# Two cross-attention layers: the first layer's leftover scalings on Pool, its maxima and sums stored from Pool's queue and loaded a fifth of a period later

## The chip, the cores and the metric

The kernel runs on one core of a Trainium2 chip. A time is the device time of one execution in microseconds (us); for the kernel before it is the median of three runs, for one of which (the profiled execution) there is also a trace. All arithmetic is in 32-bit floats. The engines are named as in the profile: PE does matmuls (its weight loads are listed as PEld), DVE and ACT are the vector and scalar engines, POOL (GpSimd) is a third engine for elementwise work that also issues DMAs, and SP only issues DMAs. PE and DVE/ACT share the accumulators in PSUM; everything else is in SBUF or, outside the core, in DRAM.

## The reference, cut to what matters

Eight batches, 100 rows of `x` with 640 columns, and a context of 722 rows with 1024 columns, the first 77 of which are text and the other 645 "ip". Two layers, each with 20 heads of 32 columns. The first layer is

```python
q = _split_heads(hidden_states @ Wq.T, H)
k = _split_heads(text @ Wk.T, H);        v = _split_heads(text @ Wv.T, H)
out_text = _merge_heads(_attend(q, k, v, sm_scale))        # softmax over 77
k_ip = _split_heads(ip @ Wk_ip.T, H);    v_ip = _split_heads(ip @ Wv_ip.T, H)
out_ip = _merge_heads(_attend(q, k_ip, v_ip, sm_scale))    # softmax over 645
return (out_text + out_ip) @ Wo.T + bo + residual
```

The second layer has the same shape with other weights; before its ip softmax it adds one bias per row and ip token, the same for all heads, and it multiplies the ip probabilities by a mask per row.

## The kernel before, in words

**Units and periods.** A unit `u` is one layer of one batch (0 to 7 the first layer, 8 to 15 the second). It is done in five chunks `c` of four heads (4 x 32 = 128 columns, the partitions of a tile). The main loop runs over the 80 pairs `(u, c)` in `ORDER`; one turn is a *period*, 11 to 33 us long. The first layer's 40 periods run from about 406 to 1380 us; ahead of them lies a preamble with all of `q` and the text's `k` and `v`.

**What a period does.** `scores` (line 982) multiplies the four heads' `q` with their keys in two parts: columns 0 to 511 (part 0), then 512 to 721 (part 1: the last 133 ip columns, then 77 of text). Rows (the 100 queries) lie on partitions. `maxima` (L1007) and `text_maxima` (L1028) reduce on DVE, `exponentials` (L1021) run on ACT and also sum. Then `factors` (L1043 to L1047) works out the sums, their reciprocals (`rz`, L1046) and the factors `mul` of the two parts. What comes after the maxima isn't emitted at once: it is put in a list, `later`, from which `emit` takes one entry ahead of each piece of other work, and all that is left at the period's end. In the period that follows, the probabilities are transposed by PE (`transposes`, L1147), copied out of PSUM, and multiplied with the values (`values`, L1173), after which the next period's scores begin.

**Other work in the same period.** Between those steps stand pieces of *production*: the products that make keys and values of the next pair of batches (`psk`, L669, and `psv`, L639). Each is done by seven products instead of eight (`seven`): every product's PSUM bank is emptied by an addition on DVE (L209, L219, L224, L230, L235) or a copy on ACT (L204, L213), and two banks are there for them. Their results (`ko`, `vo`) go out to DRAM by DMAs that Pool issues (`k_d`, L693 and L696; `v_d`, L654). `between(n, a, b, small)` emits the production that is planned between the fractions `a` and `b` of period `n`, with the small pieces in `small` (output and query projections) spread in it; `at[0]` to `at[3]` are a period's lists of those.

**What is special in the first layer.** Of the 722 columns, the first 384 (`KT` = 3 blocks of 128) are exponentiated only for their sums. Their transposed probabilities are made again in the next period, without a transpose: `key_scores` (L1123) multiplies keys with queries the other way round, `key_exponentials` adds the row maximum on DVE (L1130) and exponentiates on ACT (L1135). For that, each query's maximum must lie along the free axis of all partitions, and the same holds for the reciprocal sum, by which `values` multiplies at the end (L1179). So `finished` writes rows 8 and 9 of the small tile `st` (maxima and reciprocal sums, 100 partitions x 8 numbers) to DRAM, `st_d`, by one DMA of SP (L1075), and `load_stats` reads them back in the next period, broadcast, by five DMAs of SP (L1111 once, L1113 four times), into columns of `p` that nothing else reads. The other columns, 384 to 721, are scaled in `finished` by three DVE multiplications: 384 to 511 (L1069), 512 to 644 (L1061) and 645 to 721 (L1057), and are transposed in the next period: blocks 3 and 4 at four tenths of it, block 5 near its end.

**What sets the order.** The instructions of PE, DVE and ACT run in the order in which the program emits them (`PINNED`). Those of SP and Pool are ordered by a scheduler that knows what each waits for; each queue then runs in its order, and an instruction that waits holds up what is behind it. The loop around the change, as far as it is needed:

```python
first = last and last[0] < B          # the period before was one of layer 0
if first:
    load_stats(*last)
between(n, 0.0, 0.4, at[0])
if last:
    transposes(*last, KT if first else 0)
    transposes(*last, KT + 1 if first else 1)
between(n, 0.4, 0.5 if first else 0.6, at[1])
...
scores(u, c, 1, last if first else None)      # with key_scores of the period before
```

Of the kernel before, what the change touches and what calls it, by code (L numbers as in the profile page):

```python
# [11 lines left out]
ALU = mybir.AluOpType  # L12
AX = mybir.AxisListType

P = 128
B = 8
S = 100
# [3 lines left out]
NI = 645  # L21
NL = NI - 5 * P
NK = NI + NT
KA = 512
# [3 lines left out]
NC_ = C // P  # L28
NCC = CC // P
NTAIL = NL + NT  # L30
KT = 3
# [16 lines left out]
def two_layer_xattn(  # L48
# [17 lines left out]
    nc = tc.nc  # L66
# [20 lines left out]
    st_d = [dram.tile([2, 4, S], F32, tag=f"st_{i}", name=f"st_d{i}") for i in range(2)]  # L87
# [172 lines left out]
    with ExitStack() as es:  # L260
# [40 lines left out]
        for g in range(B // 2):  # L301
            t = fp.tile([P, 2, NC_, S], F32, tag="q", name=f"q0_{g}", bufs=2)
            ps = [product_ps(f"psq_{g}_{i}") for i in range(3)]
            for k in range(NC_):
                for c in range(NC_):
                    at = c % 2 * 2 * S
# [5 lines left out]
            for i in range(3):  # L312
                n = 2 if i < 2 else 1
# [178 lines left out]
    def load_q(u):  # L492
        l, b = divmod(u, B)
        t = tpool.tile([P, NC_, S], F32, tag="q", name=f"q_{u}")
        nc.sync.dma_start(t, q_d[l][b // 2][:, b % 2])
        qs_[u] = t

    def load_vt(u):
        l, b = divmod(u, B)
        t = tpool.tile([NTAIL, C], F32, tag="vt", name=f"vt_{u}")  # L500
        nc.sync.dma_start(t[:NL], vl_d[l][b * NL : (b + 1) * NL, :])
        nc.sync.dma_start(t[NL:], vt_d[l][b * NT : (b + 1) * NT, :])
        vts[u] = t

    def load_k(u, c):

        l, b = divmod(u, B)
        t = kpool.tile([P, NK], F32, tag="k", name=f"k_{u}_{c}")
        nc.sync.dma_start(t[:, :NI], k_d[u][:, c, :])
        nc.sync.dma_start(t[:, NI:], kt_d[l][c][:, b * NT : (b + 1) * NT])  # L510
        ks[u, c] = t

    def load_v(u, c):
        t = vpool.tile([P, NB, P], F32, tag="v", name=f"v_{u}_{c}")
        nc.sync.dma_start(t, v_d[u].rearrange("(j p) n -> p j n", p=P)[:, :, c * P : (c + 1) * P])
        vs[u, c] = t
# [457 lines left out]
    def emit(n):  # L974
        for _ in range(n):
            later.pop(0)[1]()
# [5 lines left out]
    def scores(u, c, part, keys_of=None):  # L982
# [18 lines left out]
        p, st, l = pr[u, c], stats[u, c], u // B  # L1001
        n = min(k1, NI) - k0
        lo, f, rz, mul = st[:, 8, :], st[:, 6:8, :], st[:, 9:11, :], st[:, 11:13, :]
# [38 lines left out]
        def factors():  # L1042
            nc.vector.tensor_reduce(st[:, 5, :], p[:, :, NI:], AX.X, ALU.add)  # L1043
            nc.vector.tensor_tensor(st[:, 3:5, :], st[:, 3:5, :], f, ALU.mult)
            nc.vector.tensor_tensor(st[:, 4, :], st[:, 3, :], st[:, 4, :], ALU.add)
            nc.vector.reciprocal(rz, st[:, 4:6, :])  # L1046
            nc.vector.scalar_tensor_tensor(  # L1047
                mul, f, mask_sb[:, l : l + 1], rz[:, 0:1, :].to_broadcast([S, 2, 4]), ALU.mult, ALU.mult
            )
# [5 lines left out]
        def scaled_rest(text):  # L1055
            if text:
                nc.vector.tensor_tensor(  # L1057
                    p[:, :, NI:], p[:, :, NI:], rz[:, 1, :].unsqueeze(2).to_broadcast([S, 4, NT]), ALU.mult
                )
            else:  # L1060
                nc.vector.tensor_tensor(  # L1061
                    p[:, :, KA:NI], p[:, :, KA:NI], mul[:, 1, :].unsqueeze(2).to_broadcast([S, 4, NI - KA]),
                    ALU.mult,
                )

        def finished():

            factors()
            nc.vector.tensor_tensor(  # L1069
                p[:, :, KT * P : KA], p[:, :, KT * P : KA],  # L1070
                mul[:, 0, :].unsqueeze(2).to_broadcast([S, 4, KA - KT * P]), ALU.mult,
            )
            scaled_rest(False)
            scaled_rest(True)
            nc.sync.dma_start(st_d[(NC_ * u + c) % 2].rearrange("r i q -> q r i"), st[:, 8:10, :])  # L1075

        for h in range(2):
            maxima(h)
# [29 lines left out]
    def load_stats(u, c):  # L1108

        whole, src = wholes[u, c], st_d[(NC_ * u + c) % 2]  # L1110
        nc.sync.dma_start(whole[:, :, :S], src[0].unsqueeze(0).to_broadcast([P, 4, S]))  # L1111
        for i in range(4):
            nc.sync.dma_start(  # L1113
                whole[32 * i : 32 * i + 32, :, S : S + S // 4],
                src[1, i].rearrange("(a q) -> a q", a=4).unsqueeze(0).to_broadcast([32, 4, S // 4]),
            )
# [203 lines left out]
    def loads(n):  # L1320
        u, p = divmod(n, NC_)
        if u % 2 == 0 and 0 < u <= LAST[0]:
            g = u // 2 - 1
            if p == 0 and u < LAST[0]:
                load_wo("o", wo[PAIRS[g][0] // B], g)
            if p == 1 and g < B // 2:
                load_wo("q", wq[1], g)
        if NC_ * LAST[0] + 1 <= n < NC_ * LAST[0] + 1 + NC_:
            load_wo("o", wo[1], len(PAIRS) - 2, [n - NC_ * LAST[0] - 1])
        if n == NC_ * LAST[0] + 2:  # L1330
            load_res(len(PAIRS) - 1)
        elif p == 0 and u % 2 == 1 and u < LAST[1]:
            load_res(u // 2)
        if p == 2 and u + 1 <= LAST[0]:
            load_vt(u + 1)
            load_q(u + 1)
            if u + 1 >= B:
                load_sem(u + 1)
                load_g(u + 1)
        if n == NC_ * LAST[0] - 1:  # L1340
            load_sem(LAST[1])
            load_g(LAST[1])
        if n == NC_ * LAST[0] + 1:
            load_vt(LAST[1])
        if n == len(ORDER) - 4:
            last_out_weights()

    with tc.manual_schedule(engines=PINNED):
        made_ahead = pair_tasks(PAIRS[0])
        todo = production()  # L1350
        at = pair_marks[PAIRS[0]]["k 4"] - 2
        made_ahead[at:at] = first_sums[PAIRS[1]]
        for _, f in made_ahead:
            f()
        load_q(0)
        load_vt(0)
        load_k(0, 0)
        done = [0]

        def next_task():  # L1360

            if todo[done[0]][0] and later:
                emit(1)
            todo[done[0]][2]()
            done[0] += 1

        def make(until):
            while done[0] < len(todo) and todo[done[0]][1] < until:
                next_task()

        mark = [0]

        def apart(until):

            while done[0] < len(todo) and todo[done[0]][1] < until and not any(
                t for t, _, _ in todo[mark[0] : done[0]]
            ):
                next_task()
            mark[0] = done[0]

        def between(n, a, b, small):

            mark[0] = done[0]
            near = 0.7 if n < NC_ * LAST[0] + 2 else 0.1
            for i, (_, f) in enumerate(small):
                make(n + a + (b - a) * (i + 1) / (len(small) + 1))
                apart(n + b + near)
                f()
            make(n + b)
            apart(n + b + near)  # L1390

        make(0.0)
        last = None
        for n, (u, c) in enumerate(ORDER):
            at = small_work(n)
            loads(n)
            scores(u, c, 0)
            if n == len(ORDER) - 1:
                load_v(*last)
                load_v(u, c)  # L1400
            first = last and last[0] < B
            if first:
                load_stats(*last)
            between(n, 0.0, 0.4, at[0])
            if last:
                transposes(*last, KT if first else 0)
                transposes(*last, KT + 1 if first else 1)
            between(n, 0.4, 0.5 if first else 0.6, at[1])
            if last and not first:
                transposes(*last, 2)  # L1410
                transposes(*last, 3)
            scores(u, c, 1, last if first else None)
            if n == NC_ * LAST[0] - 1:
                load_q(LAST[1])
            few = n >= NC_ * LAST[0] + 4
            if not few:
                between(n, 0.5 if first else 0.6, 0.8, at[2])
            if n < len(ORDER) - 2:
                load_v(u, c)
            if n + 1 < len(ORDER):  # L1420
                load_k(*ORDER[n + 1])
            if last:
                if not first:
                    transposes(*last, 4)
                transposes(*last, 5)
            if few:
                between(n, 0.6, 0.8, at[2])
            between(n, 0.8, 1.0, at[3])
            emit(len(later))
            if last:  # L1430
                values(*last)
            last = (u, c)
        last_out(0, [NC_ - 1])
        for j in range(6):
            transposes(*last, j, at_end=True)
        last_out_add(0)
        values(*last)
        last_out(1, [NC_ - 1])
        last_out_add(1)
# [46 lines left out]
```

## Time and profile before

| | |
|---|---|
| median of three runs | 2072.13 us (2071.38 to 2072.56) |
| the profiled execution | 2071.46 us, of which the span from first to last instruction 2069.7 |
| PE | 2023.6 us busy, 98% of the span |
| DVE | 1174.0 us, 57% |
| ACT | 716.0 us, 35% |
| POOL | 274.9 us, 13% (issuing DMAs and a few elementwise instructions) |
| the three scalings L1069, L1061, L1057 | 0.693, 0.708 and 0.471 us each; 40, 40 and 40 times in the first layer (the last two also in the second) |
| SP's write of `st_d` (L1075) | 40 times, 0.3 us to issue |
| SP waiting for that write to land, ahead of L1111 | 266.5 us in 40 waits, the longest 9.5 |

A line of the profile names a group of instructions by engine, line of the kernel, operation, and the tiles that it writes and reads. A timeline line begins with start and duration in us; in brackets stands how long the engine was idle before and what ended that. A time of PE's matmuls has a modelled end. In the lines of stretches, the columns are the stretch, its length, the busy time of PE, PEld, DVE, ACT and POOL with the number of instructions, the granted clock of PE, the DMA engines' share and GB/s. A group's line ends with count, busy time, mean duration in ns, and the idle time ahead of it with its main releasers.

### The profile page before, as it was taken

The numbers are of one execution on the slowest core, as the hardware profiler recorded it, in microseconds if no ns is written. First come the engines' busy times: TensorE is split into PE (matmuls) and PEld (weight loads), VectorE is DVE, ScalarE is ACT, GpSimd is POOL, SyncE is SP. The second block draws the span as 40 slices with busy tenths as digits, with TensorE's granted clock in tenths as the row PEclk, the third lists the DMA queues.
The fourth block names the chain that finished last, engine by engine and source line by source line (L and its number), as shares of the span: only waits on it lengthen the run. The fifth ranks groups of instructions, "written<-read, shape, count | busy, mean of one in ns | idle before, by whom it ended". The sixth has DMA issues, their size and how long they took to land.

```text
span 2069.7 us, 40047 instructions
## 1 busy us (share of the span) xinstructions
PE 2023.6 (98%) x15642; PEld 1560.7 (75%) x15642; DVE 1174.0 (57%) x3127; ACT 716.0 (35%) x2125; POOL 274.9 (13%) x433
## 2 busy tenths in 40 slices
PE   9999999999999999999999989999999999999998
PEld 9676767776776867778667867777777778889876
DVE  2223322256565465655657656655665667778787
ACT  1001000123333232223322333334544455566675
POOL 0002212111111111111111000101010101111110
PEclk9999999999999999999999999999999999999999
DMA  9544323334543755437466564536242536545461
GB/s 341 154 132 147 96 74 95 94 87 91 121 106 79 173 104 120 99 98 164 103 150 156 136 136 107 120 102 187 88 128 81 150 93 174 146 134 153 120 185 52
DMA packets 373050, 262.66 MB, mean 127 GB/s; under 512 B 123198, under 2 KB 342002, under 8 KB 372862
## 3 DMA queue, kind: packets, MB, share of 16 engines
q1 hardware_dynamic: 350814, 191.57, 38.2%
q0 software_dynamic: 21776, 68.44, 9.8%
q8 instruction: 123, 2.02, 0.5%
q14 instruction: 65, 0.53, 0.1%
q10 hardware_dynamic: 272, 0.10, 0.0%
HBM read 190.98 MB, written 69.06 MB: 126 GB/s over the span
## 4 chain that ended last, share of the span: by engine, by line
PE 60%; DVE 6%; DMA 3%; ACT 2%; issue 1%; SPq 0%; ACTq 0%; DVEq 0%
PE psv_d L639 5%; PE psv_a L639 5%; PE pspt L1147 5%; PE psk_a L669 5%; PE sc L996 5%; PE psk_d L669 4%; PE pv L1173 4%; PE pso L906 3%; PE psv_e L639 3%; PE psv_c L639 2%; PE psk_b L669 2%; PE psk_c L669 2%; PE psv_b L639 2%; PE psk_e L669 2%; PE psq L925 1%; DMA st_d<-st 1%
## 5 line engine op out<-in xcount | busy, mean ns | idle before, releaser
L1021 ACT ACTIVATE p<-sc,st 100x512 f32<-100x512 f32 (+1 forms) x320 | 165.9, 531 | 207.4 <-DVE st L1007 194.6
L1021 ACT ACTIVATE p<-p,st 100x512 f32<-100x512 f32 (+1 forms) x320 | 177.4, 556 | 75.7 <-DVE st L1013 75.6
L639 PE MATMUL psv_a<-wv,x 128*128 128x397 f32 (+1 forms) x560 | 185.5, 473 | 0.4 <-DVE ko L230 0.3
L639 PE MATMUL psv_d<-wv,s 128*128 128x320 f32 (+1 forms) x560 | 176.4, 458 | 3.4 <-ACT vo L213 2.3
L1154 DVE COPY pt<-pspt 128x400 f32<-128x400 f32 x239 | 132.9, 568 | 71.8 <-PE pspt L1147 69.7
L1147 PEld LDWEIGHTS pspt<-ident,p 100*128 100x128 f32 (+1 forms) x1440 | 141.9, 137 | 37.4 <-issue 4.9
L1147 PE MATMUL pspt<-ident,p 100*128 100x100 f32 (+1 forms) x1440 | 162.4, 251 | 6.9 <-DVE pt L1154 2.1
L693 POOL DMA_DIRECT2D k_d<-ko x140 | 100.3, 720 | 469.8 <-DVE ko L230 401.5
L1007 DVE TENSOR_REDUCE st<-sc 100x2 f32<-100x1024 f32 (+1 forms) x160 | 125.2, 824 | 54.1 <-PE sc L1123 39.6
L639 PEld LDWEIGHTS psv_a<-wv,x 128*128 128x128 f32 x560 | 103.4, 190 | 67.1 <-issue 10.4
L1013 DVE CUSTOM_DVE_ANT_0 p<-sc,sem 100x512 f32<-100x512 f32 (+1 forms) x320 | 138.7, 491 | 22.1 <-PE sc L996 20.5
L639 PEld LDWEIGHTS psv_d<-wv,s 128*128 128x128 f32 x560 | 104.4, 191 | 55.3 <-ACT vo L213 3.0
L669 PE MATMUL psk_d<-s,wk 128*128 128x256 f32 (+1 forms) x672 | 137.6, 350 | 6.0 <-DVE ko L224 4.0
L996 PE MATMUL sc<-k,q 32*100 32x210 f32 (+1 forms) x1280 | 139.9, 502 | 3.2 <-DMA k<-k_d 2.2
L669 PE MATMUL psk_a<-x,wk 128*128 128x256 f32 (+1 forms) x672 | 135.7, 347 | 1.8 <-ACT ko L204 1.0
L1135 ACT ACTIVATE pt<-pt 128x600 f32<-128x600 f32 x80 | 55.8, 705 | 228.7 <-DVE pt L1130 228.7
L669 PEld LDWEIGHTS psk_d<-s,wk 128*128 128x128 f32 x672 | 108.0, 189 | 27.1 <-DVE ko L224 5.4
L1152 ACT COPY pt<-pspt 128x400 f32<-128x400 f32 x121 | 59.5, 492 | 191.6 <-PE pspt L1147 191.5
L669 PEld LDWEIGHTS psk_a<-x,wk 128*128 128x128 f32 x672 | 109.1, 189 | 20.4 <-issue 4.2
L654 POOL DMA_DIRECT2D v_d<-vo x70 | 38.9, 556 | 634.6 <-DVE gst L629 320.3
L1053 ACT ACTIVATE p<-p,st 100x512 f32<-100x512 f32 x158 | 102.9, 715 | 27.4 <-DVE st L1047 27.1
L639 PE MATMUL psv_e<-wvt,x 128*128 128x397 f32 (+1 forms) x280 | 93.1, 474 | 0.0
(225 smaller groups left out, 3544.8 us busy)
## 6 DMA issues: line engine op xcount, KB each, us to landing
x<-ip_t SPq DMA_DIRECT2D x80, 512.0 KB
k<-k_d SPq DMA_DIRECT2D x80, 322.5 KB
v<-v_d SPq DMA_DIRECT2D x80, 320.0 KB
v_d<-vo POOLq DMA_DIRECT2D x70, 320.0 KB, 2.8
k_d<-ko POOLq DMA_DIRECT2D x112, 128.0 KB, 5.2
o<-wo SPq DMA_DIRECT2D x35, 320.0 KB
x<-ip_t SPq DMA_DIRECT2D x20, 532.0 KB
p<-st_d SPq DMA_DIRECT2D x40, 200.0 KB
```

The costliest lines, as they stand in the source:

```text
L639: nc.tensor.matmul(ps[:, :m], lhsT=tokens(k)[:, :P], rhs=w[:, k, :], start=(k == 0 and not go_on), stop=(k == HK - 1), skip_group_check=True,)
L669: nc.tensor.matmul(ps[:, i * m : (i + 1) * m], lhsT=w[:, k, :], rhs=tokens(k), start=(i == 0 and k == 0 and not go_on), stop=(k == HK - 1) ...
L693: nc.gpsimd.dma_start(dst[:, :, r], src)
L906: nc.tensor.matmul(ps[:, :cols], lhsT=wos["o", g, c][:, k, :], rhs=hsg[g][:, :n, k, :], start=(k == 0), stop=(k == NC_ - 1),)
L996: nc.tensor.matmul(scs[i // 2][:S, i % 2, : k1 - k0], lhsT=qs_[u][rows, c, :], rhs=ks[u, c][rows, k0:k1], start=True, stop=True)
L1007: nc.vector.tensor_reduce(st[:, part, 2 * h : 2 * h + 2], scs[h][:S, :, :n], AX.X, ALU.max, negate=True)
L1013: nc.vector.tensor_tensor_reduce(out=p[:, i, k0 : k0 + n], in0=scs[h][:S, i % 2, :n], in1=sems[u][:, k0 : k0 + n], scale=-1.0, scalar=3.0e ...
L1021: nc.scalar.activation(dst, dst if l else scs[h][:S, i % 2, :n], AF.Exp, bias=st[:, part, i : i + 1], scale=-1.0 if l else 1.0, accum_out= ...
L1053: nc.scalar.activation(p[:, i, :KA], p[:, i, :KA], AF.Copy, scale=mul[:, 0, i : i + 1])
L1147: nc.tensor.transpose(ps[:rows, i * S : (i + 1) * S], pr[u, c][:, i, j * P : j * P + rows], ident[:S, :S])
L1154: nc.vector.tensor_copy(dst, src)
L1173: nc.tensor.matmul(ps[32 * i : 32 * i + 32, q0 : q0 + S], lhsT=lhs, rhs=pt[:rows, j, i * S : (i + 1) * S], start=(j == 0 or apart and j == ...
```

## The change

In `finished`, which only the first layer uses, the three multiplications go from DVE to Pool; the DMA that writes the maxima and reciprocal sums to DRAM goes from SP's queue to Pool's, ahead of the multiplications. In the main loop, the five loads of `load_stats` are emitted after the production of the period's first fifth and the first small piece, instead of at the period's start. Nothing else differs, and the second layer is untouched.

```diff
         def finished():

             factors()
-            nc.vector.tensor_tensor(
-                p[:, :, KT * P : KA], p[:, :, KT * P : KA],
-                mul[:, 0, :].unsqueeze(2).to_broadcast([S, 4, KA - KT * P]), ALU.mult,
-            )
-            scaled_rest(False)
-            scaled_rest(True)
-            nc.sync.dma_start(st_d[(NC_ * u + c) % 2].rearrange("r i q -> q r i"), st[:, 8:10, :])
+            nc.gpsimd.dma_start(st_d[(NC_ * u + c) % 2].rearrange("r i q -> q r i"), st[:, 8:10, :])
+            for a, b, by in ((KT * P, KA, mul[:, 0, :]), (KA, NI, mul[:, 1, :]), (NI, NK, rz[:, 1, :])):
+                nc.gpsimd.tensor_tensor(
+                    p[:, :, a:b], p[:, :, a:b], by.unsqueeze(2).to_broadcast([S, 4, b - a]), ALU.mult
+                )
...
             first = last and last[0] < B
             if first:
+                between(n, 0.0, 0.2, at[0][:1])
                 load_stats(*last)
-            between(n, 0.0, 0.4, at[0])
+                between(n, 0.2, 0.4, at[0][1:])
+            else:
+                between(n, 0.0, 0.4, at[0])
```

## The prediction

> **What bounds the kernel now.** I read the page first, for the share of each engine, then busy time by stretches, then the timeline around each stop of PE in the first layer, then the waits of SP's own queue, and last the rows of Pool.
>
> ```profile
> span 2069.7 us, 40047 instructions
> PE 2023.6 (98%) x15642; PEld 1560.7 (75%) x15642; DVE 1174.0 (57%) x3127; ACT 716.0 (35%) x2125; POOL 274.9 (13%) x433
> ```
>
> PE bounds the whole. A change that leaves its matmuls alone, as this one does, can win only PE's idle time, and only where the first layer runs, about 406 to 1380 us. The stretches show how much that is; the second figure is PE's busy time:
>
> ```profile
> 400.00:700.00 300.00, 292.20 (x2146) 214.15 (x2145) 170.34 (x399) 89.04 (x287) 45.82 (x75) 1.00 0.41 96
> 700.00:1000.00 300.00, 296.26 (x2258) 222.05 (x2257) 173.60 (x405) 94.16 (x302) 41.33 (x66) 1.00 0.55 128
> 1000.00:1180.00 180.00, 174.69 (x1394) 134.16 (x1393) 114.19 (x254) 54.95 (x174) 23.71 (x38) 1.00 0.58 130
> 1180.00:1310.00 130.00, 120.39 (x966) 90.55 (x965) 77.89 (x180) 43.44 (x141) 11.81 (x18) 0.97 0.58 129
> 1310.00:1380.00 70.00, 69.25 (x584) 52.69 (x583) 47.70 (x125) 27.83 (x90) 6.15 (x10) 1.00 0.46 115
> ```
>
> Idle is 7.80 + 3.74 + 5.31 + 9.61 + 0.75 = 27.2 us. That is the most that can be won, 1.3%. What the moved DVE work has to do with it is seen in the timeline at 810 us:
>
> ```profile
> 810.25 0.70 DVE L1069 TENSOR_TENSOR p<-p,st 100x512 f32<-100x512 f32 x1
> 810.85 0.71 DVE L1061 TENSOR_TENSOR p<-p,st 100x532 f32<-100x532 f32 x1
> 811.48 0.47 DVE L1057 TENSOR_TENSOR p<-p,st 100x308 f32<-100x308 f32 x1
> 811.86 0.42 DVE L224 TENSOR_TENSOR ko<-psk_d,ko 128x256 f32<-128x256 f32 x1
> ...
> 812.34 2.00 PE L669 MATMUL psk_d<-s,wk 128*128 128x256 f32 x8 [1.66 <-DVE ko L224]
> ```
>
> The three scalings stand in DVE's order ahead of the addition that empties a product's PSUM bank, and PE stops until that addition is done.
>
> **Part 1, DVE loses the three scalings.** A period loses 0.693 + 0.708 + 0.471 = 1.87 us of DVE, 40 periods 75 us. Nearly all lies beside PE work and is worth nothing. What counts are the stops where the releaser stands right behind the three. I looked at every stop over 0.35 us: 1.09 us at 447 (L219), 0.61 at 472 (L235), 1.09 at 543 (L219), 0.58 at 568 (L235), 1.66 at 812 and 1.67 at 1061 (L224), 1.11 at 1275 (the copy L1154). At 1240 the scores wait 0.95 us for exponentials whose maxima L1007 stood behind the same three. All eight are under 1.87, so all should close: **-8.8 us**. The other stops follow the key exponentials (L1130, L1135) or ACT and stay.
>
> **Part 2, Pool gets them.** The rows that Pool has:
>
> ```profile
> L693 POOL DMA_DIRECT2D k_d<-ko x140 | 100.3, 720 | 469.8 <-DVE ko L230 401.5 <-issue 28.1 <-ACT pt L1135 15.6
> L696 POOL DMA_DIRECT2D k_d<-ko x80 | 43.2, 543 | 148.9 <-ACT ko L213 83.3 <-DVE ko L224 43.0 <-DVE ko L230 11.4
> ...
> L130 POOL TENSOR_TENSOR wvt<-wvt,wv 128x308 f32<-128x308 f32 x4 | 3.4, 845 | 1.2 <-DMA wvt<-text_t 1.1
> ...
> L950 POOL TENSOR_TENSOR res<-res,bias_sb 128x500 f32<-128x500 f32 x2 | 2.4, 1242 | 10.0 <-DMA res<-x_d 10.0
> ```
>
> 308 elements took 0.845 us, 500 took 1.02 and 1.47. For 512, 532 and 308 elements I take 1.2, 1.3 and 0.85: 3.4 us a period, 134 us in all on an engine that is 13% busy. In front of them stands the new DMA issue. L696 makes 128 pieces in 0.543 us, L693 256 in 0.720; on that slope 800 pieces of 4 bytes (100 partitions x 8) take 0.72 + 544/128 x 0.177 = 1.47 us. No row has such pieces. The lower end is 0.72, if pieces are free; the upper is 8 x 0.543 = 4.3, if each of the eight pieces of a partition costs a DMA of its own. I take 1.5, on the slope.
>
> So, counted from the end of the reciprocal (L1046), the first scaled block is there after 1.5 + 1.2 = 2.7 us and the second after 4.0; now they are there after 1.0 and 1.6. From the trace, the first transpose that reads them comes 7 to 16 us after the reciprocal in 37 periods, 4.6 in two (745 and 994 us), and 1.9 in one:
>
> ```profile
> 1235.51 0.51 PE L1147 MATMUL pspt<-ident,p 100*128 100x100 f32 x4
> ...
> 1236.24 0.53 PE L1147 MATMUL pspt<-ident,p 100*128 100x100 f32 x4 [0.22 <-DVE hs L1183]
> ...
> 1246.05 1.47 DVE L1130 TENSOR_TENSOR pt<-sc,p 128x600 f32<-128x600 f32 x2 [2.31 <-DMA p<-st_d]
> ...
> 1248.63 4.11 PE L639 MATMUL psv_d<-wv,s 128*128 128x320 f32 x8 [2.10 <-ACT vo L213]
> ```
>
> There the reciprocal ends at 1233.63, the second set of transposes wants its block 2.6 us later and gets it after 4.0: **+1.4 us**, once. Behind Pool's five microseconds the `k_d` and `v_d` writes queue; they feed loads a period or more later, so I put them at nothing. If that cover is gone, a store's tile comes free 5 us late: DVE already waits 1.58 us for one at 801 and at 1050, and each would cost up to 3 us.
>
> Pool also gets in DVE's way:
>
> ```profile
> 1418.07 2.45 POOL L950 TENSOR_TENSOR res<-res,bias_sb 128x500 f32<-128x500 f32 x2 [10.02 <-DMA res<-x_d]
> 1418.23 1.41 DVE L244 TENSOR_TENSOR s<-s,x 128x512 f32<-128x512 f32 x1
> ```
>
> L244, both of whose inputs are in SBUF, takes 0.713 us elsewhere and 1.41 beside Pool; L1044 took 0.70 instead of 0.16 beside L130. In the first layer 12 such DVE instructions, in 9 periods, fall where Pool would scale. At 0.5 us each that is 6 us of DVE, of which I let a quarter reach PE: **+1.5 us** (0 to 6).
>
> **Part 3, the maxima and sums.** Now:
>
> ```profile
> SPq L1111 <- DMA st_d<-st: 266.5, 40, 9.5
> ```
>
> SP issues the write (0.3 us) and then stands up to 9.5 us until it has landed; everything else that SP loads is behind it. From the reciprocal to the landing it is 6.3 us with nothing else in flight and up to 11.4 with x loads ahead in the same queue. From Pool the pieces are the same, so I take its own quiet landing, 5.9 us behind an issue of 1.5: 7.4. The lower end is 0.72 + 1.8 (fastest `g_d` store) = 2.5, the upper 4.3 + 11 = 15. The key exponentials want the loads about 4.5 us after the landing. In 35 periods they have 1 to 13 us to spare; in five (758, 1006, 1200, 1246, 1311 us) next to nothing, with the write landing 8.0, 8.0, 10.6, 8.5 and 11.4 us after the reciprocal. At 7.4 each is earlier: the 2.10 us stop at 1248 shrinks by 1.1, **-1.1 us**. At 1204 PE waits 4.13 us for a weight load that SP issued only when the write at 1185 had landed; 3.2 us earlier would help, and I count half, **-1.6 us**. Asking for the loads a fifth of a period later (3 to 6 us) adds nothing where the landing comes later still, and elsewhere eats a reserve that is there.
>
> The Trainium skill (DMA: Bandwidth & Descriptors, "Issuing engines are not separate DMA queues") says that DMAs from SP, ACT and Pool share the same 16 engines and that another issuer saves only issue time. The spread from 6.3 to 11.4 us speaks for waiting in one queue instead; by the page the last two terms would vanish and the sum be -5.9.
>
> **Sum:** -8.8 + 1.4 + 1.5 - 1.1 - 1.6 = -8.6 us against the profiled execution's 2071.46 (span 2069.7 and 1.8 around it): 2062.9. The median of the runs is 0.7 above that execution, so **2063.5 us**.
>
> **The rivals.**
> *Slower: Pool's issue is the bound.* If the 800 small pieces take Pool 4.3 us, the second block comes at 6.8 us: late by 4.2 at 1236, and by 1.8 each at 750 and 999, where the second set stands 5.0 us after the reciprocal. The landing comes at 10.2, 2 us late for three of the five tight periods. 4.2 + 3.6 + 6 + 1.5 (DVE) - 8.8 = +6.5: 2078.6. It decides from an issue of about 3.2 us, where the first three terms come to 7.3. For it: no row of Pool shows 4-byte pieces. Against it: the slope of the rows.
> *No change: the stops come back elsewhere.* PE waits also on ACT's copies behind the exponentials (1.01 us at 659 and 908). If half of the eight reopen there and the DMA terms come to nothing: -4.4 + 2.9 = -1.5: 2070.6. That the later load changes nothing, because SP's order isn't pinned and a load goes out when it can, belongs here: it takes only the DMA terms away, 2066.2.
> *A larger gain.* If SP is freed altogether, the stops at 482 (1.12), 1117 (2.23), 1204 (4.13) and 1248 (2.10) close too: -8.8 - 9.6 + 2.9 = -15.5: 2056.6.
>
> **How the numbers follow.** The forecast has 0.46, the larger gain 0.13, no change 0.18, slower 0.23. A difference of 0.2%, 4.1 us, is about what a measurement can tell from none (the three runs lie 1.2 us apart). Faster 0.59, same 0.18, slower 0.23. The range, 2055 to 2077, leaves out some of the larger gain and half of the slower case; the forecast's own is 2059 to 2067.
>
> **What would show it.** Right: DVE busy about 75 us less, Pool about 190 us more; the stops at 447, 543, 812 and 1061 gone; Pool's issue of `st_d` near 1.5 us; SP's wait for it well under 266 us. Wrong: that issue over 3.2 us, transposes waiting for Pool, or L1130 waiting for its loads in more than five periods.

## The result, and the profile after

The changed kernel takes 2077.18 us (median of 17 runs, 2070.04 to 2082.13), the kernel before on the same chip 2071.3 us (17 runs, 2068.47 to 2076.55). The ratio is 1.0028, 95% interval [1.0018, 1.0038]: slower by 0.28%, some 6 us. The prediction was 2063.5 us and faster.

The profiled execution took 2075.7 us, with a span of 2073.9, 4.2 over that of before. From the page, the busy time of each engine:

```profile
span 2073.9 us, 40377 instructions
PE 2022.6 (98%) x15642; PEld 1561.7 (75%) x15642; DVE 1121.5 (54%) x3007; ACT 714.8 (34%) x2125; POOL 433.4 (21%) x593
```

DVE is 120 instructions and 52.5 us lighter, not 75. The three scalings' listed times overlap at their ends, so that without them the trace of before is only 65 us lighter; the other 12 us are work of DVE's that has become slower. Pool has 158.5 us more. The same five stretches as before, PE's busy time being the second figure:

```profile
400.00:700.00 300.00, 296.44 (x2175) 219.82 (x2174) 156.13 (x365) 92.04 (x296) 92.71 (x123) 1.00 0.43 99
700.00:1000.00 300.00, 293.19 (x2240) 218.40 (x2240) 157.19 (x367) 93.31 (x297) 88.23 (x114) 1.00 0.56 125
1000.00:1180.00 180.00, 169.03 (x1358) 128.87 (x1357) 101.40 (x220) 52.03 (x165) 53.20 (x66) 0.99 0.56 126
1180.00:1310.00 130.00, 119.61 (x947) 91.75 (x947) 70.65 (x167) 44.42 (x142) 35.23 (x42) 0.96 0.64 134
1310.00:1380.00 70.00, 69.55 (x610) 52.71 (x608) 42.86 (x114) 24.78 (x78) 17.20 (x21) 1.00 0.51 106
```

PE's idle time is 3.56 + 6.81 + 10.97 + 10.39 + 0.45 = 32.2 us, 5.0 more than before. It fell by 4.2 in the first stretch and rose by 3.1 in the second and 5.7 in the third. So the relief came as forecast until about 690 us (a period that began at 617.3 us begins at 611.6 now), and was then given back: by 1119 us the kernel was 2 us late, by 1385 us 4.1.

Two things in the trace could have taken it. One is Pool in DVE's way, in the timeline at 806 us:

```profile
805.41 1.04 POOL L1069 DMA_DIRECT2D st_d<-st  x1 [10.80 <-DVE st L1047]
806.36 3.42 DVE L244 TENSOR_TENSOR s<-s,x 128x532 f32<-128x532 f32 x1
806.47 2.74 POOL L1071 TENSOR_TENSOR p<-p,st 100x512 f32<-100x512 f32 x3
...
810.18 1.27 PE L639 MATMUL psv_a<-wv,x 128*128 128x397 f32 x3 [2.41 <-DVE ko L230]
```

L244 took 0.71 us before. It starts just ahead of Pool's first scaling and ends after the third; the product behind it stops PE for 2.41 us, where the three scalings on DVE had stopped it for 1.66. The same happens at 1062.

The other is the write of maxima and sums. SP's waits, at the place where it stands until that write has landed:

```profile
SPq L1109 <- DMA st_d<-st: 430.8, 36, 41.0
```

The figure takes in the time in which SP formerly waited for the reciprocal, so it is to be read by period. SP's first load behind the write goes out 9.9 us after the reciprocal on average (7.7 to 13.8), where before it was 7.9 (6.2 to 11.4). Pool's issue took only 1.05 us, in most periods 0.3 us after the reciprocal; the 14 landings that the trace shows came 8.7 us (median) after the issue began. The key additions (L1128) wait for the loads 11.3 us in 8 periods, before 4.3 in 4. The longest of these waits, from the write to the stop of PE:

```profile
1256.34 1.06 POOL L1069 DMA_DIRECT2D st_d<-st  x1 [1.74 <-DVE st L1047]
...
1265.63 0.37 SPq L1109 DMA_DIRECT2D p<-st_d  x1
...
1269.85 1.47 DVE L1128 TENSOR_TENSOR pt<-sc,p 128x600 f32<-128x600 f32 x2 [4.09 <-DMA p<-st_d]
...
1271.24 0.41 DVE L219 TENSOR_TENSOR ko<-psk_c,ko 128x256 f32<-128x256 f32 x1
1271.71 3.78 PE L669 MATMUL psk_d<-s,wk 128*128 128x256 f32 x8 [4.61 <-DVE ko L219]
```

and the same period before:

```profile
1251.49 0.30 SPq L1075 DMA_DIRECT2D st_d<-st  x1
...
1266.98 1.47 DVE L1130 TENSOR_TENSOR pt<-sc,p 128x600 f32<-128x600 f32 x2
...
1268.99 2.00 PE L669 MATMUL psk_d<-s,wk 128*128 128x256 f32 x8 [0.52 <-DVE ko L219]
```

The loads go out 9.6 us after the reciprocal, before 8.8. But DVE is now ready for the key additions 9.7 us after the reciprocal, where before it came to them after 15.5. The split of the small pieces does that: the runs below that have it with the write on another queue stop here too, 2.0 to 3.4 us (c, l, j, m, k), and Pool's later landing makes it 4.61.

### The profile page after: what moved, and what is told of

It is laid out like the page before. It is cut to its first block, busy times and chain, and to the rows that moved or that the text cites. A ratio compares the mean times of both kernels' runs of the same rounds, so it can differ in the third digit from the quotient of the medians.

```text
span 2073.9 us, 40377 instructions
## 1 busy us (share of the span) xinstructions
PE 2022.6 (98%) x15642; PEld 1561.7 (75%) x15642; DVE 1121.5 (54%) x3007; ACT 714.8 (34%) x2125; POOL 433.4 (21%) x593
## 4 chain that ended last, share of the span: by engine, by line
PE 60%; DMA 5%; DVE 4%; issue 3%; ACT 1%; POOL 0%; SPq 0%; POOLq 0%; DVEq 0%; ACTq 0%
PE psv_a L639 6%; PE pspt L1145 5%; PE sc L996 5%; PE psk_a L669 5%; PE psv_d L639 5%; PE psk_d L669 5%; PE pv L1171 4%; PE psv_e L639 3%; PE psv_c L639 2%; PE pso L906 2%; PE psk_c L669 2%; PE psv_b L639 2%; PE psk_b L669 2%; DMA st_d<-st 2%; PE psk_e L669 2%
## 5 line engine op out<-in xcount | busy, mean ns | idle before, releaser
L639 PEld LDWEIGHTS psv_a<-wv,x 128*128 128x128 f32 x560 | 104.4, 191 | 71.1 <-issue 10.9
L1013 DVE CUSTOM_DVE_ANT_0 p<-sc,sem 100x512 f32<-100x512 f32 (+1 forms) x320 | 138.7, 490 | 22.3 <-PE sc L996 20.7
L996 PE MATMUL sc<-k,q 32*100 32x210 f32 (+1 forms) x1280 | 139.4, 504 | 4.8 <-DMA k<-k_d 4.8
L1071 POOL TENSOR_TENSOR p<-p,st 100x512 f32<-100x512 f32 (+2 forms) x120 | 114.5, 988 | 0.7
```

What stands on the lines that cost most here:

```text
L639: nc.tensor.matmul(ps[:, :m], lhsT=tokens(k)[:, :P], rhs=w[:, k, :], start=(k == 0 and not go_on), stop=(k == HK - 1), skip_group_check=True,)
L996: nc.tensor.matmul(scs[i // 2][:S, i % 2, : k1 - k0], lhsT=qs_[u][rows, c, :], rhs=ks[u, c][rows, k0:k1], start=True, stop=True)
L1013: nc.vector.tensor_tensor_reduce(out=p[:, i, k0 : k0 + n], in0=scs[h][:S, i % 2, :n], in1=sems[u][:, k0 : k0 + n], scale=-1.0, scalar=3.0e ...
L1071: nc.gpsimd.tensor_tensor(p[:, :, a:b], p[:, :, a:b], by.unsqueeze(2).to_broadcast([S, 4, b - a]), ALU.mult)
```

## The experiments

In the table, "loads" is the mean time from the reciprocal to SP's first load of maxima and sums, "key wait" what the key additions waited for them in all, and "windows" the number of 3.41 us windows of half clock that PE got in the first layer (more on these below). These three are from one profiled execution each, the ratio from all runs. Each ratio is to the kernel before as it ran on the same occasion; there were five of these beside the result's own: a to d; e to g; h, i, l and j; i2, k, m and n; the last three. That kernel's own median was 2075.3, 2064.8, 2072.7, 2064.8 and 2074.5 us on them, and the second and the third were on the same chip. So two ratios from different occasions can be compared less closely than their intervals say.

| kernel | scalings | write | small pieces | ratio to before, 95% | loads, us | key wait, us | windows |
|---|---|---|---|---|---|---|---|
| before | DVE, one block | SP | whole | 1 | 7.9 | 4.3 | 2 |
| before, again | DVE, one block | SP | whole | 0.9996 [0.9985, 1.0007] | 8.3 | 6.9 | 4 |
| changed | Pool | Pool | split, late load | 1.0028 [1.0018, 1.0038] | 9.9 | 11.3 | 4 |
| a_pool_scales | Pool | SP | whole | 0.9962 [0.9949, 0.9974] | 8.3 | 7.8 | 3 |
| b_pool_writes | DVE, one block | Pool | whole | 1.0049 [1.0030, 1.0068] | 10.0 | 13.2 | 6 |
| c_late_load | DVE, one block | SP | split, late load | 0.9961 [0.9945, 0.9976] | 8.4 | 4.4 | 2 |
| d_early_load | Pool | Pool | whole | 1.0033 [1.0020, 1.0046] | 10.1 | 15.6 | 9 |
| e_no_scaling | none | SP | whole | 0.9946 [0.9934, 0.9959] | 7.3 | 3.6 | 1 |
| f_dve_spread | DVE, spread | SP | whole | 0.9962 [0.9946, 0.9977] | 7.4 | 1.7 | 1 |
| g_dve_next | DVE, next period | SP | whole | 0.9966 [0.9953, 0.9980] | 7.4 | 1.2 | 0 |
| h_act_writes | DVE, one block | ScalarE | whole | 1.0011 [0.9997, 1.0024] | 7.9 | 4.9 | 2 |
| i_sp_delayed | Pool | SP, of a copy by Pool | whole | 0.9956 [0.9940, 0.9972] | 8.4 | 8.1 | 5 |
| i2_sp_late | Pool | SP, 4 us late | whole | 1.0081 [1.0068, 1.0093] | 10.9 | 20.5 | 5 |
| l_split_only | DVE, one block | SP | split, early load | 0.9959 [0.9946, 0.9972] | 8.0 | 3.5 | 5 |
| j_a_late | Pool | SP | split, late load | 0.9933 [0.9921, 0.9945] | 8.1 | 3.9 | 2 |
| m_pool_act_late | Pool | ScalarE | split, late load | 0.9950 [0.9937, 0.9962] | 7.3 | 2.5 | 1 |
| k_f_late | DVE, spread | SP | split, late load | 0.9933 [0.9919, 0.9946] | 7.3 | 1.5 | 2 |
| n_two_writes | DVE, one block | SP, and Pool for nobody | whole | 1.0055 [1.0043, 1.0068] | 7.6 | 4.6 | 5 |
| q_pool_100 | DVE, one block | SP, and Pool in 100 pieces for nobody | whole | 0.9993 [0.9981, 1.0004] | 8.2 | 4.5 | 3 |
| r_act_800 | DVE, one block | SP, and ScalarE for nobody | whole | 0.9997 [0.9985, 1.0009] | 9.1 | 5.8 | 3 |

### One part at a time

**Pool scales, SP writes** (a): the scalings as in the change, and ahead of them SP's own write; the main loop as before. Against d, that is one word:

```diff
-            nc.gpsimd.dma_start(st_d[...].rearrange("r i q -> q r i"), st[:, 8:10, :])
+            nc.sync.dma_start(st_d[...].rearrange("r i q -> q r i"), st[:, 8:10, :])
```

> Pool does the three scalings; the write of the maxima and sums stays on SP and comes first, the loads stay where they were. Theory 1 (two losses: Pool's three multiplications in a row hold up DVE's two-input additions, and the write from Pool's queue lands about 2 us later): the relief of 8.8 us on DVE stays, the contention of some 3 to 5 us stays, the late landing is gone: 4 to 6 us under before (2065 to 2068). The 2.4 us stops behind L230 at 810 and 1062 are still there, the stops at 1114 and 1267 are not longer than before. Rival A (contention is the whole loss): 3 to 6 us over before. Rival B (the write's landing is the whole loss): 8 us or more under before. Rival C (the later load and the split of the small pieces are the loss): 7 to 9 us under before as well, then the kernel with the main loop's change alone is slower.

**Pool writes, DVE scales** (b): only that line of the change, the other way round.

> Only the write moves to Pool's queue; the scalings stay on DVE, the loads stay where they were. Theory 1: the landing comes some 2 us later than from SP after the reciprocal (about 9.8 instead of 7.7 us), which costs the key exponentials' reserve in some periods: 3 to 8 us over before (2074 to 2079), with longer waits of the key additions L1128/L1130 for their loads. Rival A (contention is the whole loss): within 2 us of before. Rival C (later load and split): within 2 us of before.

**The main loop alone** (c), and **the change without the main loop's part** (d):

```diff
             if first:
+                between(n, 0.0, 0.2, at[0][:1])
                 load_stats(*last)
-            between(n, 0.0, 0.4, at[0])
+                between(n, 0.2, 0.4, at[0][1:])
+            else:
+                between(n, 0.0, 0.4, at[0])
```

> Only the main loop's change: the loads of maxima and sums a fifth of a period later, and the small pieces of the first two fifths emitted in two parts. Scalings on DVE and write on SP as before. Theory 1: within 2 us of before, since a later place of these loads in SP's order matters only where the landing is early. Rival C: 4 to 8 us over before, because the split changes the order of the small production pieces on PE, or because the loads now stand behind others in SP's order.

> The changed kernel with the main loop's change undone: Pool scales and writes, the loads stand where they did before. Theory 1: as the changed kernel, 4 to 7 us over before. Rival C: 0 to 8 us under before, at least 5 under the changed kernel.

Measured: a 0.9962, c 0.9961, b 1.0049, d 1.0033. Two of the three parts are gains of about 8 us each, and the third, the write from Pool's queue, is a loss: of 0.49% by itself (b), of 0.71% from a to d, which differ in nothing but the issuer, on one occasion. The contention is not the loss: a has Pool's three scalings and is faster. Rival C has it the wrong way round, since the main loop's part gains by itself; theory 1 had expected nothing of it.

What a late landing does to SP's other loads is seen in d, at its longest stop. SP's queue, Pool's write and the scores of part 0, in the timeline of d:

```profile
1327.48 1.05 POOL L1069 DMA_DIRECT2D st_d<-st  x1 [2.01 <-DVE st L1047]
1336.53 0.37 SPq L1109 DMA_DIRECT2D p<-st_d  x1
1336.95 1.92 SPq L1111 DMA_DIRECT2D p<-st_d  x4
1338.98 0.39 SPq L176 DMA_DIRECT2D x<-ip_t  x1
1339.47 2.31 SPq L529 DMA_DIRECT2D gt<-g_d  x1
...
1344.03 0.87 SPq L509 DMA_DIRECT2D k<-k_d  x1
...
1356.88 2.04 PE L996 MATMUL sc<-k,q 32*100 32x512 f32 x8 [7.67 <-DMA k<-k_d]
```

and the same period in the trace of before:

```profile
1316.65 0.30 SPq L1075 DMA_DIRECT2D st_d<-st  x1
...
1323.63 0.37 SPq L1111 DMA_DIRECT2D p<-st_d  x1
...
1330.05 1.37 SPq L509 DMA_DIRECT2D k<-k_d  x1
...
1338.65 1.12 PE L996 MATMUL sc<-k,q 32*100 32x512 f32 x8
```

Both are of the same period. From the write's issue to SP's first load it is 9.1 us in d and 7.0 before; to the load of the keys 16.6 and 13.4. That load has nothing to do with maxima and sums: it stands behind them in SP's queue, and the next scores wait for it. Its later issue accounts for at most 3.2 of the 7.67 us. The rest comes from the load itself: the scores start 12.9 us after its issue, before 8.6 and without a wait, and 7.1 in i2 (below) at the same place. Pool's next write, issued at 1349.20, was in flight meanwhile; that it held the load up is not shown. What PE then loses is more than the stop, as d's stretches show (PEclk stands ahead of the DMA share):

```profile
1346.00:1350.00 4.00, 3.21 (x56) 2.15 (x54) 3.44 (x12) 2.21 (x12) 2.11 (x3) 1.00 1.13 285
1350.00:1354.00 4.00, 0.00 (x0) 0.00 (x0) 0.07 (x1) 0.00 (x0) 2.98 (x4) 0.72 0.83 115
1354.00:1358.00 4.00, 1.12 (x8) 0.45 (x8) 0.00 (x0) 0.00 (x0) 0.00 (x0) 0.50 0.44 34
1358.00:1362.00 4.00, 4.00 (x14) 2.16 (x7) 2.36 (x2) 1.45 (x4) 0.00 (x0) 0.50 0.23 22
1362.00:1366.00 4.00, 4.00 (x17) 2.76 (x17) 0.90 (x2) 1.90 (x6) 0.00 (x0) 1.00 0.30 49
```

When PE stands, the granted clock falls to one half and stays there for 10.2 us, about 5 of them after the matmuls have begun again. In d there are nine windows of 3.41 us at half clock in the first layer, before two. Its first layer, 20.7 us longer by the profile, has 14.5 us more idle time and 6.2 us more of PE at work.

**Relief without Pool.** The kernel without the scalings (e), and two in which DVE does them, but not in one block (f, g). In f each scaling is an entry of its own in the list `later`; in g these entries may wait until the next period.

```diff
                 later.append((False, finished))
+                later.append((False, lambda: nc.vector.tensor_tensor(
+                    p[:, :, KT * P : KA], p[:, :, KT * P : KA],
+                    mul[:, 0, :].unsqueeze(2).to_broadcast([S, 4, KA - KT * P]), ALU.mult,
+                )))
+                later.append((False, lambda: scaled_rest(False)))
+                later.append((False, lambda: scaled_rest(True)))
```

> The three scalings of the rest of p are left out altogether, so neither DVE nor Pool does them; the write stays on SP, the loads where they were. This is the relief of DVE by itself. Theory 1: 8 to 10 us under before (about 2062), with the stops at 447, 472, 543, 568, 812, 1061 and 1275 gone. Rival D (the stops come back elsewhere, the relief is worth nothing): within 3 us of before; then even a free Pool could not have made the change pay.

> The scalings stay on DVE, but no longer in one block of 1.9 us: they are three entries of the list of work that is spread over the period's later part, and the write of maxima and sums goes out on SP ahead of them. Theory 1: most of the relief without Pool: the stops of about 1.1 to 1.7 us behind the block shrink to at most one scaling (0.7 us) and the write starts 1.9 us earlier: 4 to 8 us under before. Rival D: within 3 us of before. If the transposes come to wait for scalings that are late, up to 5 us over before.

> As the kernel with the scalings spread on DVE, except that they may fall into the next period, just ahead of the transposes that read them. Theory 1: 3 to 8 us under before if the transposes of the rest of p find their blocks ready; if they wait, PE stops up to 0.7 us in each of 40 periods, and it is up to 20 us over before.

e came to 0.9946, 11 us; f to 0.9962 and g to 0.9966, 8 and 7 us. So the relief is real, and Pool isn't needed for most of it: breaking up the block of 1.87 us on DVE gains as much as moving it to Pool (a).

### Is it the issuer, the lateness, or the queue?

**ScalarE's queue writes** (h): the kernel before with `nc.scalar.dma_start` for the write. **SP's write delayed** (i): Pool copies the maxima and sums between its second and third scaling, and SP writes the copy.

> As the kernel before, only that ScalarE's queue issues the write of maxima and sums instead of SP's; scalings on DVE, loads where they were. This leaves SP as free as Pool's write does, but without Pool's queue. Theory 1 (what costs is that a write from Pool's queue lands 2 to 3 us later, and that SP stands until it has landed): it lands about as soon as SP's (6 to 8 us after the reciprocal), and the time is within 4 us of before, or better. Rival B2 (what costs is that SP no longer issues the write, which moves its other loads): 6 to 12 us over before, as with the write on Pool.

> Pool scales and SP writes, as in the first experiment, but the write is of a copy that Pool makes after the first two of its three scalings, so that it starts about 2.3 us after the reciprocal instead of at once. Nothing is written from Pool's queue. Theory 1: the lateness alone does the harm: the landing comes 2 to 2.5 us later, SP's loads behind it too, and most of the 15 us between the first experiment (8 us under before) and the one with Pool's write and early loads (7 us over) comes back: 2 to 8 us over before. Rival B2 or B3 (Pool's queue itself does the harm, by its issue or by the stores of keys and values that stand behind it): within 3 us of the first experiment, 5 to 11 us under before.

h is 1.0011 with an interval that holds 1, and its loads go out as early as before: freeing SP of the write does nothing that these runs can tell. i did not do what it was meant to. The copy depended on the reciprocal alone and went out ahead of the scalings, so that SP's write was 0.35 us late in most periods instead of 2.3. It is a repeat of a, and agrees with it (0.9956); one thing follows all the same, that an instruction of Pool which waits for the reciprocal costs nothing there.

**The delay by a true dependence** (i2): the copy adds zeros made from a scaled value.

```diff
+                if b == NI:
+                    nc.gpsimd.tensor_tensor(st[:, 13, :], p[:, :, NI - 1], p[:, :, NI - 1], ALU.subtract)
+                    nc.gpsimd.tensor_tensor(
+                        st[:, 0:2, :], st[:, 8:10, :], st[:, 13, :].unsqueeze(1).to_broadcast([S, 2, 4]), ALU.add
+                    )
...
+            nc.sync.dma_start(st_d[...].rearrange("r i q -> q r i"), st[:, 0:2, :])
```

> Pool scales and SP writes, but a copy that Pool can make only when the second of its scalings is done (it adds a difference of one scaled value with itself), so that the write starts about 2.5 us after the reciprocal. No write from Pool's queue. Theory 1 (the lateness of the landing does the harm): the loads' issue moves from 8.3 to about 10 us after the reciprocal, as with Pool's write, and the time lies 8 to 15 us over that of the version with Pool scaling and SP writing at once, 0 to 7 us over before. Rival B3 (Pool's DMA queue does the harm): as that version, 5 to 10 us under before, however late the landing.

The write started 4.0 us after the reciprocal, more than meant, and the loads at 10.9 us, 2.6 later than in a. The ratio is 1.0081, 17 us over before, where theory 1 had 0 to 7. By the ratios that is 1.19% or 25 us over a, by the times themselves (2080.1 and 2067.5, on different occasions) 13. No write of Pool's is in it. So a late landing is enough to do harm of the size that was seen. But it does it by another way than the stop of d: PE waits for keys (L996) only 1.2 us in all, while the key additions, and DVE's work behind them, wait most of all the runs, 20.5 us. In the kernels with Pool's write PE waits for keys 4.8 us (changed), 9.8 (b) and 12.5 (d), in before 2.2 and in a 3.4.

**A second write that nobody waits for**: from Pool (n), from Pool in 100 pieces of 32 bytes (q), from ScalarE (r); beside them the kernel before once more.

```diff
+            nc.gpsimd.dma_start(sx_d[(NC_ * u + c) % 2].rearrange("r i q -> q r i"), st[:, 8:10, :])
```

> The kernel before, with Pool writing the same 800 pieces a second time, into a place that nobody reads; SP's own write, the scalings on DVE and the loads are as before. Theory 1: nobody waits for Pool's write, so within 4 us of before, if SP's write lands as it did. Rival B3 (Pool's queue does the harm by its issue, its packets or the stores behind it): 7 to 12 us over before.

> The kernel before, with a second write of the same 3,200 bytes from Pool's queue to a place that nobody reads, laid out so that each partition is one piece of 32 bytes: 100 pieces instead of 800. Theory 3a (the pieces cost: Pool's write of 800 took the DMA engines 17 us each time, SP's 7): within 3 us of before. Theory 3b (the issue from Pool's queue costs, whatever the pieces): 6 to 12 us over before, as with 800 pieces.

> The kernel before, with the second write of 800 pieces issued from ScalarE's queue instead of Pool's. Theory 3a: the pieces cost the DMA engines less than half of what they cost from Pool's queue (7 us against 17), so 2 to 6 us over before. Theory 3b: within 2 us of before.

> The kernel before once more, with nothing changed but a comment: within 2 us of before by every theory. Its trace is wanted from the same chip.

n is 1.0055, against theory 1, which had it within 4 us: Pool's 800 pieces cost 11 us even when nobody waits for them. q is 0.9993 and r 0.9997, both no change. By the ratios, then, it is neither a write from Pool as such nor 800 pieces as such, but the two together. This is not fully shown: n ran on the occasion on which the kernel before took 2064.8 us, q and r on the one with 2074.5, and neither was run on the other's; in us, n (2075.8) is only 1.6 above q (2074.2). What the write hits isn't settled either. The rows of the DMA queues, with the time that packets took as a share of the 16 engines, of n:

```profile
q0 software_dynamic: 23696, 68.65, 11.9%
```

and of r:

```profile
q0 software_dynamic: 21776, 68.44, 10.6%
q10 hardware_dynamic: 32672, 0.23, 1.5%
```

Pool's queue (q0) had 9.8% in before, and theory 3a took n's 17 us for each write from the difference, 2.1% of 16 x 2070.7 us. That difference isn't the write's alone: r's row has 10.6% with the same 21776 packets as before, so the time of Pool's other stores varies too. Packet by packet, one write of Pool's is 16 packets of 256 bytes (383 ns on average), 16 of 64 (67 ns) and 16 of 4 in n's trace, 7 us in all. The same numbers written by ScalarE are 810 packets (in r's row 32672 less the 272 of before, by 40) of 4 bytes: 7 us too in h, 12 in r. So the engines' time doesn't tell the cases apart, theory 3a was right on q only and 3b on r only. But the trace doesn't have the pieces alike: 48 packets a write from Pool, a third of them 383 ns long, against 810 of 9 ns in h.

### The change with another issuer, and the best versions

**The split without the late load** (l): the loads first, then both parts of the small pieces, all else as before. **a with the main loop's part** (j); **f with it** (k); **the change with ScalarE's queue for the write** (m), one word of it:

```diff
-            nc.gpsimd.dma_start(st_d[...].rearrange("r i q -> q r i"), st[:, 8:10, :])
+            nc.scalar.dma_start(st_d[...].rearrange("r i q -> q r i"), st[:, 8:10, :])
```

> Only the split of the small pieces into two parts, with the loads of maxima and sums where they were before, ahead of both. The later load together with the split gained 8 us. Theory 2a (the gain is the load's place: what SP would otherwise hold back behind the wait for the write goes out first): within 3 us of before. Theory 2b (the gain is the order of the small pieces on PE): 5 to 9 us under before.

> Pool scales, SP writes first, and the loads come a fifth of a period later: the change with its write left on SP. Theory 1: the two gains come largely from different stops (the additions behind the scalings; SP's loads behind the write), so 10 to 16 us under before. If they are the same idle time of PE: 6 to 9 us under before, as each alone.

> The scalings stay on DVE as three entries spread over the period, SP writes ahead of them, and the small pieces are split with the loads a fifth later. The best version that the runs so far point to: 8 us from the spread and 4 to 8 from the split, 10 to 16 us under before. If both gains are the same idle time of PE: 6 to 9 us under before.

> The change with one word different: ScalarE's queue issues the write instead of Pool's; Pool scales, the loads come later. Theory 1: as the version with SP's write (12 us under before), within 4 us, so some 17 us under the changed kernel. If freeing SP is what harms: 0 to 6 us over before.

l gains what c gains (0.9959 and 0.9961), so it is the order of the small pieces that gains, and the loads' place is worth nothing that these runs can tell. j is 0.9933, 0.29% better than a, so most of both gains add up. m is 0.9950: with one word changed, the change is 10 us faster than before instead of 6 slower. Its stretches in the same places:

```profile
700.00:1000.00 300.00, 297.19 (x2282) 221.24 (x2281) 157.28 (x375) 92.87 (x297) 78.30 (x102) 1.00 0.52 126
1000.00:1180.00 180.00, 177.43 (x1440) 138.29 (x1439) 106.48 (x236) 57.16 (x183) 47.40 (x63) 1.00 0.60 143
1180.00:1310.00 130.00, 123.95 (x1039) 94.93 (x1038) 72.45 (x172) 47.08 (x149) 30.53 (x37) 0.99 0.55 125
```

PE is idle 2.8 + 2.6 + 6.1 = 11.4 us there, the changed kernel 28.2. The best are j and k, both 0.9933, 14 us under before. k leaves Pool out altogether, so Pool is not what makes the change pay.

## Why the prediction was wrong

The runs give the parts their sizes: Pool's scalings 0.9962, the main loop's part on top of that 0.9933, and Pool's write in place of SP's on top of both 1.0028 / 0.9933 = 1.0096. In us of 2071.3 that is -7.9, -6.0 and +19.8, +5.9 in all. (These ratios are from three occasions; within one, c has -8 us for the main loop's part and d against a +15 for the write.)

- **Part 1, the relief: right.** -8.8 was forecast, e measured -11 (-8.5 to -13.6). The stops at 447, 472, 543, 568, 1240 and 1275 are gone in the changed kernel, all eight in e. The three hold DVE for some 1.6 us a period, not 1.87, since their times overlap; no term hung on the difference, as all eight closed.
- **Part 2, Pool's scalings: right in sum, one mechanism too small.** +2.9 was forecast; from e to a it is 0.16%, 3 us, within what the two intervals leave open. The scalings took 2.96 us a period (3.35 forecast). The transposes of the 1236 us place wait for Pool 0.47 us in a, not 1.4. The contention was taken as 0.5 us for each DVE instruction; L244 was held through three of Pool's in a row, 2.7 us. This depends on where the scalings fall: behind the write's issue, in the changed kernel, the two stops at 810 and 1062 are 2.41 us; without it, in a, they are 0.80 and 0.79 (809 and 1057).
- **Part 3, the write: this is the step that failed,** with its sign. It stood at -2.7 us (-1.1 and -1.6) and is +10 by itself, +20 at the end. The sum took SP's landing, 5.9 us behind the issue, for a write from Pool ("the pieces are the same"). The trace counts 48 packets for Pool's write and 810 for SP's. The issue was cheaper than forecast, 1.05 us for 1.5, but the landing came 8.7 us after the issue began, where the sum had 1.5 + 5.9 = 7.4. SP's loads went out at 9.9 us on average instead of 7.4, and in the five tight periods at 8.8, 8.2, 11.3, 8.2 and 11.6 us: none reached 7.4, and four of them are later than before. The second half of the step was wrong as well: a landing was priced by the five tight periods and one weight load. In the changed kernel the key additions wait in eight periods, the longest one (1270) not among the five: the split had eaten its reserve, a cost that the prediction named ("eats a reserve that is there") and did not price. PE's waits for keys grew too (2.2 to 4.8 us, 12.5 in d). And n shows a cost of the write that no reading of a wait would have found.
- **A third term was missing:** what a stop does to the clock. The profile and the stretches of before had it (0.97 in the fourth stretch), and no sum used it. The Trainium skill (TensorE: Matmul & The Clock Gate, "Part 1: The HAM clock gate (the "warmup" mystery)") says that the clock is gated to one half by windows of activity some 3.4 us long; the traces agree on the length, with dips of 3.41, 6.83 and 10.24 us in the first layer and nothing between. The skill has the drop come after an idle window of that length; here a stop of 2.10 us (at 1248 in before) was followed by one. A window at half clock costs PE up to 1.7 us, half of 3.41.
- **The main loop's part was read only as the place of the loads.** For that, "adds nothing" was right (l against c). The split of the small pieces that comes with it gains 8 us by itself and was not priced. Which of the reordered pieces does it was not tried.
- **The rivals.** The slower one gave 2078.6, close to the result, but by an issue of over 3.2 us and transposes that wait for it; the issue was 1.05. It decided nothing. Its landing at 10.2 us was close to what came, by another route.
- **The Trainium skill's rule that was weighed against the trace** (DMA: Bandwidth & Descriptors, "Issuing engines are not separate DMA queues"), by which another issuer saves only issue time: SP and ScalarE agree with it (h, 1.0011), Pool's 800 pieces do not (b, 1.0049), and the error is on neither of the two sides that were weighed.

What stays open: how the 20 us divide between the late landing and the unawaited cost of n. Each by itself can cost as much as b did (10): i2 and n took them one at a time. No run took the lateness out of Pool's write. A part can be read from the traces of the changed kernel and of j, which differ by the issuer alone: PE is idle 12 us more in the changed kernel. 3.2 of them are the two stops beside Pool's scalings, which the write's issue pushes back by 1 us; the stop at 1271 has 1.3 more than in j, and the rest lies in stops of which none is over 2.1 us longer.

A caution on single traces: the kernel before, run again on another occasion, had an execution of 2076.4 us, with stops at 1117 and 1251 of 2.8 and 3.0 us where the first trace has 2.2 and 2.1, and four half-clock windows instead of two. It also has a stop of 1.41 us at 1318 that the first trace lacks, behind a DVE addition that stood behind a wait for loads. The stops that depend on transfers move by so much with nothing changed; those behind the block of scalings (1.09 twice at 447, 1.66 and 1.65 at 812, 1.67 and 1.64 at 1061) are the same within 0.03 us. A forecast from one trace is safe for the second kind alone.

## What to carry to other kernels

When a queue stands until a write has landed, price the landing for all that is behind that queue, and don't carry a landing time from one issuer to another: in this kernel a small write in hundreds of tiny pieces did well on SP's or ScalarE's queue and badly on Pool's. Add to a stop of PE of some 2 us or more the half-clock windows that may follow it. And before work is moved to another engine, try breaking it up where it is: here three separate scalings on DVE gained what Pool's did.

## What the runs showed of the hardware

- A write of 800 pieces of 4 bytes, made 40 times from Pool's queue instead of SP's, costs this kernel 0.49% (b), from ScalarE's queue nothing that 12 runs can tell (h). With nobody waiting for it, it cost 11 us (n, 0.55%); the same bytes in 100 pieces from Pool, or the 800 pieces from ScalarE, cost nothing that 12 runs can tell, on another occasion (q, r).
- The trace has 48 packets for one such write from Pool, the largest of 256 bytes, and 810 of 4 bytes from SP or ScalarE; the DMA engines' time is about 7 us for each (n, h).
- Pool issued it in 1.05 us, less than the slope of its other rows gave (1.5), and it landed 8.7 us (median of 14) after the issue began.
- A DVE addition with both inputs in SBUF, 0.71 us by itself, took 3.42 us beside three Pool multiplications in a row (2.74 us): its time is that of all three and its own, not of one.
- The granted clock falls to one half in windows of 3.41 us. A stop of 7.67 us (d) came with three of them in a row; of the stops of 2 to 3 us some came with one or two (2.10 at 1248 in before, 2.98 at 1251 in its second trace) and some with none (2.23 at 1117 in before, 2.41 at 810 in the changed kernel).
